# Layer 0 of a four-layer convolution network: loads written into the expansion, and the convolution's own patch on array tiles of 64 rows by 32 columns

## The chip, the cores and the metric

The kernel runs on one core of a Trainium2 chip. The metric is the device time in microseconds (us) of the whole kernel, which computes four layers one after the other. Only layer 0 is changed, and in the trace its blocks lie between about 147 and 4060 us of 6624. All data are fp32.

## The reference, cut to what matters

The input is `x` of shape (4, 64, 256, 256). Layer 0 adds to it the following function of its group-normalised self. Layers 1 to 3 are not touched.

```python
x = jnp.einsum('bchw,oc->bohw', x, w_in)              # 64 -> 384 channels
xp = patches of 8 x 8 of x
xp = jnp.fft.irfft2(jnp.fft.rfft2(xp) * fft_filter)   # per channel and patch
x = lax.conv_general_dilated(x, w_dw, 3 x 3, padding 1, feature_group_count=C)
x1, x2 = jnp.split(x, 2, axis=1)
x = jax.nn.gelu(x1, approximate=False) * x2
return jnp.einsum('bchw,oc->bohw', x, w_out)          # 192 -> 64 channels
```

The filter of a patch and the 3 x 3 convolution are linear and per channel. So the kernel does both in one go: each output pixel of a patch is a sum over the 64 pixels of its own patch, and for pixels at two edges over some pixels of the neighbour patches.

## The kernel before

**Tiling.** A block is 11 rows of patches of one image; there are three blocks to an image and 12 in all (`blocks`, index `p`). Within a block the 384 hidden channels are taken in four quarters (`kb`). For each quarter two stages follow each other on PE.

**Expansion** (`expand`, lines L444 and L450): for each of up to 12 rows of patches (`t`) PE computes the quarter's channels into PSUM tiles `psu`, with pixels of a patch on the partitions, and ACT and DVE copy them into the SBUF tile `u` (L459 to L463). There is one `u`, so the convolution starts when the last row is copied.

**Convolution** (`convolve`, twelve groups `g` of four channel pairs): the own patch (L494) is a matmul of 64 rows by 64 columns, two row halves `h` by two column halves `c`, four array tiles at a time, moving 374 columns. Then three units (`UNITS`: 16, 28 and 4 columns; L503) add the neighbour patches, in tiles of 64 by 32, eight at a time. An fp32 matmul appears as two MATMUL and two LDWEIGHTS instructions in the trace. ACT takes the Gelu of one half (L510), DVE multiplies by the other (L511), and the POOL queue stores the product `h` to DRAM tile `g` (L514).

**Projection** (`project`, L591 with 128 by 64 tiles, then L598 with 64 by 64): sixteen units of the block before, (row `r` of a patch, half), are woven into the convolution: four to a quarter, one `unit()` each after groups 1, 4, 7 and 10. Each needs tiles `g1` and `g6` from DRAM (`load_g`, L546 and L550), and each `r` needs the residual rows (`load_r`, L559). A `unit()` projects and right after it calls `load_half` for the next `r`. Pools of two buffers each hold `g1`, `g6` and `r`.

**Order.** PE, DVE, ACT and SP run in the order in which the program is written (`manual_schedule`); each queue for itself[...]. SP issues all loads: the convolution weights (`load_w`, L471, one tile for two groups, three pairs ahead, four buffers), the halves, the next image's statistics tiles (`load_stats`, L627, and `next_stats`, bn_stats at L320), and the next block's input rows (`load_x`, L418, then `normalize_x` at L256). Statistics and input tiles share a pool of four buffers. The statistics tiles are loaded in the first three quarters after every third group; the first four input rows stand after the last group of the third quarter, the others among the groups of the fourth.

**Weights.** At the start POOL writes the 64 by 112 tables of each channel to DRAM tiles `wts`, of which `load_w` fetches four channel pairs at a time.

## Time and profile before

| | |
|---|---|
| median of 3 runs | 6649.44 us (6638.31 to 6666.61) |
| profiled execution, its time | 6626.21 us |
| its span | 6624.4 us |
| mean granted TensorE clock | 0.953 |
| PE busy | 6040.5 us, 106712 matmuls |
| instructions in all | 238282 |
| DMA packets of queue 8 (instructions) | 843, 13.81 MB |
| own patch (L494): matmuls, mean | 9216, 494 ns |
| neighbour units (L503): matmuls, mean | 27648, 483 ns |

"PE" is the matmul side of TensorE and "PEld" its weight loads. Matmuls on different array tiles overlap, so a mean of 494 ns is not the time that one takes away from the next: the distance between starts is. The share of busy time counts overlapping matmuls once.

### The profile page before, as it was taken

How to read it: one execution, taken by the hardware profiler on the slowest of the kernel's cores; microseconds unless marked ns; L12 is line 12 of the kernel's file. 1: busy time of each engine (PE TensorE's matmuls, PEld its weight loads, DVE VectorE, ACT ScalarE, POOL GpSimd, SP SyncE). 2: the span in 40 equal slices, each digit the busy share in tenths (PEclk: the TensorE clock that was granted, in tenths of full speed). 3: DMA queues.
4: the chain of work that ended last, by engine and by line, in shares of the span. 5: the costliest groups of instructions: out<-in, count | busy, mean ns of one | idle time of the engine just before them, and what ended most of it. 6: DMA issues, size and time to landing. Idle time of an engine off the chain costs nothing.

```text
span 6624.4 us, 238282 instructions
## 1 busy us (share of the span) xinstructions
PE 6040.5 (91%) x106712; PEld 3213.7 (49%) x106712; DVE 4275.7 (65%) x5924; ACT 3238.8 (49%) x4564; POOL 1050.4 (16%) x1646
## 2 busy tenths in 40 slices
PE   2999999999999999999999986999899999999987
PEld 1455555555555555555555543333344444443576
DVE  5556555555555555555555545999798898885355
ACT  4454434344434444344444422777777887783211
POOL 3111111111111111111111111111022222221011
PEclk9999999999999999999999997999999999999855
DMA  8577777777878877877767669999666666677889
GB/s 236 152 206 211 216 213 222 218 216 213 230 213 238 219 222 207 223 214 220 210 193 206 188 194 247 232 229 228 165 177 176 168 180 173 173 187 264 318 351 394
DMA packets 878510, 1447.67 MB, mean 219 GB/s; under 512 B 77252, under 2 KB 586452, under 8 KB 875444
## 3 DMA queue, kind: packets, MB, share of 16 engines
q1 hardware_dynamic: 725284, 923.09, 54.8%
q0 software_dynamic: 148672, 500.14, 21.7%
q8 instruction: 843, 13.81, 0.9%
q10 hardware_dynamic: 3536, 9.20, 0.5%
q14 instruction: 175, 1.43, 0.1%
HBM read 932.08 MB, written 500.04 MB: 216 GB/s over the span
## 4 chain that ended last, share of the span: by engine, by line
PE 82%; DMA 6%; ACT 5%; DVE 3%; issue 3%; SPq 0%; POOL 0%; ACTq 0%; DVEq 0%; POOLq 0%
PE pc L503 18%; PE pc L494 12%; PE m L869 10%; PE psu L444 9%; PE one L1110 8%; PE div L1069 6%; PE po L591 4%; ACT u L459 4%; PE psu L450 4%; PE psz L1099 2%; PE po L598 2%; DMA x<-x 2%; PE psa L1297 2%; DMA g<-g 2%; PE psy L1444 1%
## 5 line engine op out<-in xcount | busy, mean ns | idle before, releaser
L511 DVE TENSOR_TENSOR h<-h,pc 128x374 f32<-128x374 f32 x1152 | 574.7, 541 | 1268.7 <-ACT h L510 1267.7
L510 ACT ACTIVATE h<-pc 128x374 f32<-128x374 f32 x1152 | 492.6, 480 | 1824.9 <-PE pc L503 1822.0
L503 PE MATMUL pc<-u,w 64*16 64x374 f32 (+2 forms) x27648 | 1244.1, 483 | 0.0
L494 PE MATMUL pc<-u,w 64*64 64x374 f32 x9216 | 928.6, 494 | 81.1 <-DVE u L463 32.2
L514 POOL DMA_DIRECT2D g<-h x576 | 416.7, 723 | 3111.0 <-DVE h L511 2904.7
L503 PEld LDWEIGHTS pc<-u,w 64*16 64x16 f32 (+2 forms) x27648 | 413.8, 92 | 769.5 <-issue 768.9
L444 PE MATMUL psu<-win,xn 64*128 64x96 f32 x8704 | 627.0, 283 | 131.8 <-ACT u L459 110.5
L459 DVE COPY u<-psu 64x384 f32<-64x384 f32 x1088 | 604.3, 555 | 167.7 <-PE psu L444 155.7
L459 ACT COPY u<-psu 64x384 f32<-64x384 f32 x1088 | 560.0, 515 | 238.9 <-PE psu L444 218.8
L444 PEld LDWEIGHTS psu<-win,xn 64*128 64x128 f32 x8704 | 574.0, 192 | 202.6 <-ACT u L459 143.6
L1055 DVE TENSOR_TENSOR q<-xn 128x2313 f32<-128x2313 f32 (+2 forms) x256 | 627.4, 2492 | 1.7 <-ACT xn L256 1.7
L1110 PE MATMUL one<-z,wp 32*32 32x512 f32 x16384 | 592.1, 596 | 17.8 <-issue 13.6
L494 PEld LDWEIGHTS pc<-u,w 64*64 64x64 f32 x9216 | 350.3, 133 | 531.0 <-issue 354.7
L256 ACT ACTIVATE xn<-x,nb,r 128x1024 f32<-128x1024 f32 (+3 forms) x272 | 486.8, 1793 | 244.6 <-DMA x<-x 140.8
L1056 ACT ACTIVATE q<-q 128x2313 f32<-128x2313 f32 (+2 forms) x256 | 529.0, 2086 | 32.7 <-DVE q L1055 31.2
L450 PE MATMUL psu<-win,xn 64*64 64x96 f32 x17408 | 458.2, 252 | 81.9 <-issue 57.2
L1069 PE MATMUL div<-q,ones 64*32 64x512 f32 x8192 | 466.3, 594 | 12.9 <-ACT q L1056 9.3
L1110 PEld LDWEIGHTS one<-z,wp 32*32 32x32 f32 x16384 | 367.6, 103 | 223.6 <-issue 80.1
L450 PEld LDWEIGHTS psu<-win,xn 64*64 64x64 f32 x17408 | 395.5, 137 | 126.0 <-issue 77.0
L1143 POOL DMA_DIRECT2D x<-r x512 | 275.5, 547 | 969.8 <-DVE r L1140 945.1
L591 PE MATMUL po<-g,wo 128*64 128x176 f32 (+1 forms) x3072 | 315.8, 348 | 63.3 <-DMA g<-g 41.3
L869 PE MATMUL m<-t,wk 64*64 64x512 f32 x3072 | 341.1, 588 | 0.0
(162 smaller groups left out, 6668.1 us busy)
## 6 DMA issues: line engine op xcount, KB each, us to landing
g<-h POOLq DMA_DIRECT2D x576, 374.0 KB, 7.0
x<-x SPq DMA_DIRECT2D x240, 640.0 KB, 6.4
w<-wt SPq DMA_DIRECT2D x288, 448.0 KB, 8.4
x<-x SPq DMA_DIRECT2D x100, 1024.0 KB, 14.2
g<-g SPq DMA_DIRECT2D x414, 187.0 KB, 5.7
g<-g SPq DMA_DIRECT2D x736, 93.5 KB, 6.0
x<-in_x_dram SPq DMA_DIRECT2D x256, 256.0 KB, 8.1
x<-o POOLq DMA_DIRECT2D x128, 512.0 KB, 8.2
```

The lines of the kernel that those rows point to most:

```text
L444: nc.tensor.matmul(ps[s][:, k, at], xn[halves[s], n : n + 2].rearrange("p n r w -> p (n r w)"), win[halves[s], kb, 0 : 2 * PB], start=True ...
L450: nc.tensor.matmul(ps[s][halves[1 - odd], k, at], xn[halves[s], n + odd].rearrange("p r w -> p (r w)"), win[halves[s], kb, PB * (1 - odd) ...
L459: copy(at(h, 8 * s + o), v[k, c : c + PB])
L494: nc.tensor.matmul(out(C * c, C, k, h), w[halves[h], k, 2 * (G % 2) + c, 0:C], cells(h, 4 * g + 2 * k + c, 0, 0), start=True, stop=False, ...
L503: nc.tensor.matmul(out(q, m, k, h), w[halves[h], k, 2 * (G % 2) + c, c0 : c0 + m], cells(h, 4 * g + 2 * k + c, down, right), start=False, ...
L511: nc.vector.tensor_mul(h[:, k], h[:, k], ps[k][:, 1, 0:L])
L591: nc.tensor.matmul(out(k, s, x), wo1, moving(g1[:, 2 * k], 2 * half + k, s, x), start=(x == 0), stop=False, skip_group_check=True,)
L869: nc.tensor.matmul(rows2(m)[halves[j], s], w[dx][halves[s]], ts[n][halves[s], i, 2 * j : 2 * j + 2, dx : dx + W], start=(dx == 0), stop=(d ...
L1055: nc.vector.tensor_sub(d, p0, p1)
L1056: nc.scalar.activation(d, d, AF.Square)
L1069: ins = nc.tensor.matmul(ps[quarters[j], h], ones[halves[h]], q[n, g, k][halves[h], r + 2 * j : r + 2 * j + 2, o : o + W], start=(m == 0), ...
L1110: ins = nc.tensor.matmul(rows2(ps[g])[quarters[j], k], w[quarters[i]], z[quarters[i], h, 2 * j + dy : 2 * j + dy + 2, dx : dx + W], tile_p ...
```

## The change

- The own patch is computed in twice as many matmuls of 32 columns each, with a loop over the column half `q`, so that all of the convolution uses tiles of 64 by 32.
- The weight tiles in DRAM and SBUF hold the two phases `k` of a channel next to each other: a partition of `load_w` reads one run of 4 x 2 x 112 values where it read two runs of 4 x 112.
- Projection units stand after groups 0, 3, 6 and 9. After the first two, the next half is loaded at once; after the other two it is put on a list `later` and loaded in the program text of the next expansion, after its rows 7 and 9. The first halves of a block (written ahead of its first expansion so far) go the same way.
- In the expansions of the first three quarters, up to four statistics tiles are loaded after rows 8 to 11; in that of the fourth, the first four input rows. `next_stats` runs after odd groups.
- The last pass, which only projects the last block, loads as before.

```diff
-        wts = [dr.tile([2, 64, 2, Q, NC], F32, name=f"wt{t}") for t in range(HID // C)]
+        wts = [dr.tile([2, 64, Q, 2, NC], F32, name=f"wt{t}") for t in range(HID // C)]
...
-            w = wl[j] = p_w.tile([128, 2, 4, NC], F32, tag="w", name=f"w_{j}")
+            w = wl[j] = p_w.tile([128, 4, 2, NC], F32, tag="w", name=f"w_{j}")
             nc.sync.dma_start(
-                w, wts[k // 8][:, :, :, 4 * (k % 8) : 4 * (k % 8) + 4].rearrange("h i k c n -> (h i) k c n")
+                w, wts[k // 8][:, :, 4 * (k % 8) : 4 * (k % 8) + 4].rearrange("h i c k n -> (h i) c k n")
             )
...
             for k in range(2):
-                for c in range(2):
-                    for h in range(2):
-                        nc.tensor.matmul(
-                            out(C * c, C, k, h), w[halves[h], k, 2 * (G % 2) + c, 0:C], cells(h, 4 * g + 2 * k + c, 0, 0),
-                            start=True, stop=False, tile_position=(h * C, c * C), skip_group_check=True,
-                        )
+                for q in range(2):
+                    for c in range(2):
+                        for h in range(2):
+                            at = C * c + Q * q
+                            nc.tensor.matmul(
+                                out(at, Q, k, h), w[halves[h], 2 * (G % 2) + c, k, Q * q : Q * q + Q],
+                                cells(h, 4 * g + 2 * k + c, 0, 0),
+                                start=True, stop=False, tile_position=(h * C, at), skip_group_check=True,
+                            )
...
-                ahead = 1
+                ahead, later = 1, []
...
                 for r in range(ahead):
                     for half in range(2):
-                        load_half(p - 1, r, half)
-
-                def unit():
+                        later.append((p - 1, r, half))
+                        if p == NB:
+                            load_half(*later.pop())
+
+                def unit(wait=False):
                     at = next(units, None)
                     if at:
                         project(p - 1, *at)
-                        load_half(p - 1, at[0] + ahead, at[1])
+                        later.append((p - 1, at[0] + ahead, at[1]))
+                        if not wait:
+                            load_half(*later.pop(0))
...
                     for t in range(NR + 1):
                         if 0 <= i0 + t < NP:
                             expand(p, kb, t)
+                        if t in (7, 9) and later:
+                            load_half(*later.pop(0))
+                        if t >= 8:
+                            if kb == 3 and t - 8 < len(fresh):
+                                load_x(fresh[t - 8])
+                            elif kb < 3 and nk:
+                                loaded.append(nk.pop(0))
+                                load_stats(b + 1, loaded[-1])
...
-                        if g in (1, 4, 7, 10):
-                            unit()
+                        if g in (0, 3, 6, 9):
+                            unit(wait=g > 3)
                         if kb < 3:
-                            if g % 3 == 0:
-                                if len(loaded) == 2 or not nk:
-                                    for k in loaded[: 1 if nk else 2]:
-                                        next_stats(b + 1, loaded.pop(0))
-                                if nk:
-                                    k = nk.pop(0)
-                                    load_stats(b + 1, k)
-                                    loaded.append(k)
-                            if kb == 2 and g == NG - 1:
-                                for row in fresh[:4]:
-                                    load_x(row)
+                            if g % 2 and loaded:
+                                next_stats(b + 1, loaded.pop(0))
```

More of the change, by code (lines that the diff above doesn't have):

```diff
@@ L395, in weights @@
                             nc.gpsimd.dma_start(
-                                wts[t][h, 32 * hh : 32 * hh + 32, k, :, n0 : n0 + n].rearrange("i c n -> c i n"),
+                                wts[t][h, 32 * hh : 32 * hh + 32, :, k, n0 : n0 + n].rearrange("i c n -> c i n"),
                                 T[quarters[2 * h + k], :, :, c0 : c0 + n].rearrange("p a b n -> p (a b) n"),
@@ L503, in convolve @@
                             nc.tensor.matmul(
-                                out(q, m, k, h), w[halves[h], k, 2 * (G % 2) + c, c0 : c0 + m],
+                                out(q, m, k, h), w[halves[h], 2 * (G % 2) + c, k, c0 : c0 + m],
                                 cells(h, 4 * g + 2 * k + c, down, right),
```

## The prediction

> **What bounds the kernel now.** I read the page first: its busy table, its chain, its groups. Then the order of time inside one block of layer 0, then the waits of PE and of the SP queue, and last the DMA share in stretches of 4 us.

> ```profile
> PE 6040.5 (91%) x106712; PEld 3213.7 (49%) x106712; DVE 4275.7 (65%) x5924; ACT 3238.8 (49%) x4564; POOL 1050.4 (16%) x1646
> ...
> PE pc L503 18%; PE pc L494 12%; PE m L869 10%; PE psu L444 9%; PE one L1110 8%; PE div L1069 6%; PE po L591 4%; ACT u L459 4%; PE psu L450 4%; PE psz L1099 2%; PE po L598 2%; DMA x<-x 2%; PE psa L1297 2%; DMA g<-g 2%; PE psy L1444 1%
> ```

> PE is the bound, and the two lines of the convolution, L494 (own patch) and L503 (neighbour units), are 30% of the chain. Groups of the page: L503 has 27648 matmuls, L494 9216; that is 48 and 16 for each of 576 groups (12 blocks, 4 quarters of the channels, 12 groups). All of it lies between 146.6 and 3937 us. One group of the convolution in the timeline of all engines:

> ```profile
> 1500.65 1.52 PE L494 MATMUL pc<-u,w 64*64 64x374 f32 x16
> ...
> 1501.02 0.16 PEld L494 LDWEIGHTS pc<-u,w 64*64 64x64 f32 x4 [0.16 <-PE pc L503]
> ...
> 1501.33 0.17 PEld L494 LDWEIGHTS pc<-u,w 64*64 64x64 f32 x4 [0.15 <-issue]
> 1502.10 0.15 PEld L503 LDWEIGHTS pc<-u,w 64*16 64x16 f32 x16 [0.60 <-issue]
> 1502.10 2.16 PE L503 MATMUL pc<-u,w 64*16 64x374 f32 x48
> ...
> 1503.08 0.13 PEld L503 LDWEIGHTS pc<-u,w 64*4 64x4 f32 x8 [0.17 <-issue]
> 1503.40 0.13 PEld L503 LDWEIGHTS pc<-u,w 64*4 64x4 f32 x8 [0.19 <-issue]
> ...
> 1504.20 1.53 PE L494 MATMUL pc<-u,w 64*64 64x374 f32 x16
> ```

> The first column is the start. A group lasts 1504.20 - 1500.65 = 3.55 us. Its matmuls run in rounds: four at a time on tiles of 64 by 64 (4 rounds), eight at a time on tiles of 64 by 32 (6 rounds). Consecutive bursts of weight loads are 0.31 to 0.33 us apart, so (1503.40 - 1502.10) / 4 = 0.325 us is a round. Ten rounds are 3.25 us; the missing 0.30 us stand at the two seams: 1.45 us from the first L494 to the first L503, where four rounds are 1.30, and 2.10 us to the next group, where six are 1.95. So **a seam costs 0.15 us**, and PE waits for nothing else there. Now the waits of PE, the longest of the SP queue, and the DMA share (last but one column) around one expansion, which began at 1200.5 and gave way to the convolution at 1226:

> ```profile
> PE psu L444 <- ACT u L459: 110.5, 171, 1.5
> ...
> PE psu L450 <- issue: 57.2, 48, 4.2
> ...
> PE psu L444 <- issue: 18.7, 23, 1.8
> ...
> SPq L546 <- PE po L591: 1280.3, 117, 32.5
> ...
> 1208.00:1212.00 4.00, 2.53 (x82) 2.25 (x78) 3.09 (x6) 3.49 (x8) 0.00 (x0) 1.00 1.07 262
> ...
> 1216.00:1220.00 4.00, 2.92 (x56) 2.66 (x60) 2.82 (x6) 2.60 (x6) 0.00 (x0) 1.00 0.03 7
> ...
> 1228.00:1232.00 4.00, 3.83 (x36) 1.35 (x44) 0.02 (x1) 0.00 (x0) 0.00 (x0) 0.60 0.00 0
> ...
> 1268.00:1272.00 4.00, 4.00 (x76) 1.47 (x72) 1.00 (x2) 1.02 (x3) 0.73 (x1) 1.00 1.06 323
> ```

> The DMA engines are full through the convolution and the first 16 us of the expansion, then empty for some 20 us, because SP stands at L546 for a buffer that the next projection frees. The convolution waits for no load: its groups follow each other without idle time. The expansion does wait: for ACT's copies, and 71 times (48 + 23) for "issue", 75.9 us in all, none of them in the convolution.

> [...] a seam at each change of 64 by 64 to 64 by 32, of 0.15 us, and none between the three units[...]. [...] The page's queue 8 agrees on the size (843 packets, 13.81 MB; PE's 213,424 instructions are 253 to a packet); I read the "issue" waits as late blocks[...]. [...] The stretch 1228:1232 above has a granted clock of 0.60 after PE waited for the last copies[...].

> **The change part by part.**
> 1. *Own patch on tiles of 64 by 32.* It takes 32 instructions of each kind per group where there were 16 (fp32 matmuls stand twice in the trace), eight at a time: again four rounds. Bounds of a round 0.31 (own now) and 0.33; I take the units' 0.325. Of a convolution phase with four projections (44 of 48): eight own parts fall from 1.45 to 1.30, four that follow a projection from 1.41 (1509.82 to 1511.23) to 1.30, seven unit parts that run into the next group from 2.10 to 1.95. That is 1.20 + 0.44 + 1.05 = 2.69 us. Against it, L598 of the projection is itself 64 by 64, so the own part after it gets a seam that it didn't have: 4 x 0.17 = 0.68 (the first own round after a seam is 0.02 us longer). After an expansion the new seam lies under the wait for the last copies (L494 waits there 1 to 2 us anyway). Net 2.0 us; 44 x 2.0 = 88. The four phases of block 0 have no projection: 23 seams x 0.15 = 3.45, x 4 = 14. **Sum 102 us less.**
> 2. *9216 matmuls and 9216 weight loads more.* Their time is in the rounds; their fetching isn't. A group asks for 160 instructions in 3.25 us, 49 a us, where it was 128 in 3.55, 36 a us. The expansion runs at about 192 in 3.5 us, 55 a us, between its waits, and there late blocks cost 75.9 us over some 53,000 instructions, 0.36 us a block. From below: nothing, as now. From above: the expansion's price, 8.6 blocks x 0.36 = 3.1 us a phase, 137 us over 44 phases. I take 0.9 us a phase, 40 us: the rate is nearer the expansion's than to the old one, but the next step takes load off the DMA engines in these phases. **40 us more.**
> 3. *Loads moved.* Two of four half loads of a phase (1.12 MB each, every other with 0.7 MB of residual rows) and the four statistics tiles (0.5 MB each) are written after the ninth group now instead of among the groups. SP's order is only that of its own queue: nothing in it waits for the expansion's rows, so "second half" is where they stand in the text. They will issue as soon as the weight load of the eleventh group has its buffer, about 9 us before the expansion starts; the buffers that they need (g1, g6, r, x) are free by then. That is 9 us before, up to some 15 us after the start of the expansion: the stretch that is full today. Queued behind them on SP is the weight load of the next first group, due six groups later, over 20 us. The POOL queue keeps its stores and waits for none of these. The convolution loses nearly 2.2 + 0.7 + 2 MB of some 16. PE waits on no load today in these phases, so the move alone gains nothing; that projections start one group earlier finds their tiles landed (6 to 8 us to landing, a whole expansion before use). In the last of the four quarters the four x tiles stood at the same place of SP's order already. Bounds for the expansions: later statistics loads may add 1 us to each (+44), a shorter queue may take 1 us away (-44). I take 0. DVE's statistics at odd groups: 1.28 us beside 1.1 us of products in 3.25 us, and after a half 1 also some 3.3 us of projection work in 5.5: covered.
> 4. *Weight layout.* The same bytes, one run of 3584 B per partition instead of two of 1792. Loads are three pairs of groups ahead (8.4 us to landing); 0, or a little DMA time back. The table writes keep their run lengths: 0.

> Sum: -102 + 40 = -62. The profiled execution took 6626.2 us around a span of 6624.4, 23 us under the median of the three runs (6649.4), so its counterpart is 6564, and for the median 6649 - 62 = **6587**.

> **Rivals.**
> - *The fetch stays hidden and the expansions recover* (0.16). For it: the DMA queue in the convolution is shorter. Against: it carries h stores and weight loads all the same. 102 + up to 30: about 6520 to 6550.
> - *Instruction fetch becomes the bound of the convolution* (0.17), the slower side. Place: all 44 phases with projections. It decides when a block of 256 takes longer than 256 / 49 = 5.2 us under load. For it: median landings of 6 to 8 us for other transfers in the page; the late blocks of the expansion. Against: no such wait today at 7.1 us a block. Price: the expansion's 0.36 us a block gives 137 - 102 = +35; with all that the expansions lose (by their starts in the timeline 11 rows take 23.6 us and 12 rows 26.2 where nothing disturbs them; all 47 together take some 120 us more, over 209 blocks) 0.6 a block, 227 - 102 = +125. So 6684 to 6775.
> - *The change doesn't do what it says* (0.15). Either the eight weight loads of an own round keep the rounds from packing (own back at 1.45), so that only the seven seams into the next group go, or the loads stay bunched and the fetch eats most of the gain: 6625 to 6660.

> **How the numbers follow.** Likeliest (0.52): 6587, with its own range 6540 to 6625 from half to one and a half times the terms of 40 and of the expansions. The full range reaches into the first rival and into the low end of the slower one: 6500 to 6690. A measurement of this kernel can tell about 0.5%, 33 us, from no change; below 6616 lie most of the likeliest and the first rival: 0.61; within 33 us a part of the likeliest and most of the last: 0.22; above, 0.17.

> **What would show it.** Step 1: L494 64 columns gone, 18432 matmuls of 32, a group of 3.2 to 3.3 us, L598 to L494 longer by 0.15. Step 2: about 73 more packets on queue 8 and "issue" among the waits of L494 and L503, some 40 us. Step 3: SP's loads at the start of the expansion, the DMA share still near zero in its last 10 us, and the wait at L546 shorter. The forecast is wrong if the group stays at 3.5 us, if "issue" in the convolution is over 100 us, or if PE waits for g at a phase's first projection.

## The result, and the profile after

The changed kernel is slower: 6716.31 us median of 4 runs (6701.14 to 6729.94) against 6643.88 us for the kernel before, a ratio of 1.0101 (95% interval 1.0074 to 1.0128). The forecast was 6587 us, with 6690 as its upper end. The profiled execution took 6729.94 us around a span of 6728.2, 104 us more than that of before. The medians are 72 us apart: the profiled execution of before was 18 us under its median, this one 14 over. What follows on single stages is read from this pair of executions, so it adds up to 104 and not to 72.

The page, with the busy table, the chain and the instruction queue:

```profile
PE 6048.6 (90%) x115928; PEld 3620.6 (54%) x115928; DVE 4282.5 (64%) x5924; ACT 3243.7 (48%) x4564; POOL 1046.6 (16%) x1646
...
q8 instruction: 915, 14.99, 1.0%
...
PE pc L506 17%; PE pc L496 12%; PE m L875 10%; PE psu L444 9%; PE one L1116 9%; PE div L1075 7%; PE psu L450 4%; PE po L594 4%; ACT u L459 4%; PE po L601 2%; PE psz L1105 2%; DMA x<-x 2%; PE psa L1303 2%; DMA g<-g 1%; PE psy L1450 1%
```

PE is busy for nearly the same time as before with 9216 matmuls more (the own patch is L496 now, the units L506, the projection L594 and L601), and queue 8 moved 72 packets more. An undisturbed stretch of the convolution, in the timeline of PE (start, duration, line, forms, count):

```profile
1509.20 1.53 PE L496 MATMUL pc<-u,w 64*32 64x374 f32 x32
1510.48 2.16 PE L506 MATMUL pc<-u,w 64*16 64x374 f32 x48
1512.40 1.53 PE L496 MATMUL pc<-u,w 64*32 64x374 f32 x32
1513.66 2.19 PE L506 MATMUL pc<-u,w 64*16 64x374 f32 x48
1515.58 1.58 PE L496 MATMUL pc<-u,w 64*32 64x374 f32 x32
1516.84 2.28 PE L506 MATMUL pc<-u,w 64*16 64x374 f32 x48
1519.05 1.46 PE L594 MATMUL po<-g,wo 128*64 128x160 f32 x16
1520.44 0.85 PE L601 MATMUL po<-g,wo 64*64 64x160 f32 x16
1521.22 1.54 PE L496 MATMUL pc<-u,w 64*32 64x374 f32 x32
```

From one L496 to the next are 3.20 and 3.18 us where it was 3.55: **the seams are gone**. So the loss is elsewhere. The waits of PE (in total, times, longest), with one line of the SP queue:

```profile
PE psu L450 <- issue: 100.3, 76, 3.3
PE psu L444 <- ACT u L459: 93.0, 150, 0.9
...
PE pc L506 <- issue: 35.5, 31, 3.1
...
PE psu L444 <- issue: 30.2, 23, 3.4
...
PE pc L496 <- issue: 23.9, 19, 2.1
...
SPq L549 <- PE po L594: 1095.2, 88, 24.4
```

"issue" has come into the two lines of the convolution and has grown in the expansion's two from 75.9 to 130.5 us. What one such wait does is seen in the fourth quarter of one block:

```profile
1989.38 0.88 PE L450 MATMUL psu<-win,xn 64*64 64x96 f32 x29
1993.34 1.86 PE L450 MATMUL psu<-win,xn 64*64 64x96 f32 x35 [3.09 <-issue]
1995.13 3.73 PE L444 MATMUL psu<-win,xn 64*128 64x96 f32 x32
2000.88 3.22 PE L496 MATMUL pc<-u,w 64*32 64x374 f32 x32 [2.02 <-DVE u L459]
2003.34 3.95 PE L506 MATMUL pc<-u,w 64*16 64x374 f32 x48
...
2050.32 1.13 PE L496 MATMUL pc<-u,w 64*32 64x374 f32 x17
2052.11 0.56 PE L496 MATMUL pc<-u,w 64*32 64x374 f32 x8 [0.66 <-issue]
...
2055.93 1.79 PE L506 MATMUL pc<-u,w 64*16 64x374 f32 x32
2058.98 0.85 PE L506 MATMUL pc<-u,w 64*4 64x374 f32 x15 [1.25 <-issue]
```

PE stands in the middle of a row for 3.09 us; then the same 32 matmuls of L444 that take 2.03 us elsewhere (at 1982.94, for instance) take 3.73, and after the wait for DVE's copies the units take 3.95 instead of 2.2. The clock goes with that. The same expansion in stretches of 4 us (the last three columns are granted clock, DMA share and GB/s):

```profile
1987.00:1991.00 4.00, 3.01 (x61) 2.72 (x61) 3.47 (x7) 3.31 (x7) 0.00 (x0) 1.00 1.14 207
1991.00:1995.00 4.00, 1.66 (x35) 1.57 (x35) 0.73 (x2) 0.48 (x1) 0.00 (x0) 0.74 0.60 98
1995.00:1999.00 4.00, 3.86 (x35) 3.49 (x32) 1.74 (x4) 1.59 (x4) 0.00 (x0) 0.50 0.00 0
```

The DMA engines are full (a share of 1.14), PE stands, and then the clock is halved (0.50).

The trace itself supports reading these waits as late instruction blocks. Queue 8 moved 915 packets of 16,384 bytes each, and PE's 234,284 instructions in the trace (matmuls, weight loads and its sequencer's own) are 256 to a packet. The wait above ended at 1993.34 us, 1.58 us after such a packet had ended at 1991.76. Of the 153 "issue" waits in the two stages of layer 0, 151 end 1.2 to 1.8 us after the end of a packet of queue 8; of 20,000 random moments, 9% do, and of the 223 waits for other causes, 5%. And all 153 stand at the same place in PE's program: the number of these instructions that PE had started is the same modulo 256, to within 2. In the kernel before it is so for all 71 (70 of them at that distance from a packet).

The fourth quarter of that block as a whole, before (two lines) and after (two lines), expansion and convolution in turn:

```profile
1931.50:1959.00 27.50, 20.73 (x520) 18.87 (x513) 22.71 (x42) 20.80 (x41) 1.23 (x2) 1.00 0.88 193
1959.00:2013.40 54.40, 53.98 (x900) 22.62 (x900) 21.40 (x40) 20.65 (x33) 11.55 (x16) 0.97 0.85 224
```

```profile
1965.70:2000.90 35.20, 24.85 (x514) 22.71 (x514) 22.36 (x41) 20.73 (x41) 0.71 (x1) 0.84 0.84 193
2000.90:2059.80 58.90, 55.49 (x1092) 30.27 (x1092) 20.84 (x35) 20.87 (x33) 12.60 (x16) 0.95 0.91 245
```

By the starts of the stages in the timelines, the mean length of a stage in blocks 1 to 11 (in the fourth quarter 1 to 10), in us:

| quarter | expansion before | after | convolution before | after | "issue" in it after |
|---|---|---|---|---|---|
| first | 26.5 | 26.9 | 52.9 | 53.2 | 0.9 |
| second | 27.4 | 28.8 | 52.8 | 51.5 | 0.0 |
| third | 26.9 | 28.0 | 53.7 | 52.0 | 0.2 |
| fourth | 28.7 | 32.1 | 53.6 | 59.4 | 4.9 |

Over all stages but the last convolution and its tail: expansions 1319 to 1394 us (+75), convolutions 2466 to 2491 (+25). The sum, 100, is nearly the whole of the 104. "Issue" in them went from 76 to 131 us and from 0 to 66. The length of the half clock times one half, which is the most that it can have cost, went from 61 to 140 us (by the clock records of the traces, which hold full speed and 0.5 of it and nothing else). The waits and the clock overlap with waits that were there anyway, for instance for ACT's copies (110 to 93 us for L444), so they don't add up exactly.

### The profile page after: what moved, and what is told of

It reads as the page before. It is cut to its first block, busy times and chain, and to the rows that moved or that the text cites. A ratio compares the mean times of both kernels' runs of the same rounds, so it can differ in the third digit from the quotient of the medians.

```text
span 6728.2 us, 256613 instructions
## 1 busy us (share of the span) xinstructions
PE 6048.6 (90%) x115928; PEld 3620.6 (54%) x115928; DVE 4282.5 (64%) x5924; ACT 3243.7 (48%) x4564; POOL 1046.6 (16%) x1646
## 4 chain that ended last, share of the span: by engine, by line
PE 82%; DMA 5%; ACT 4%; issue 4%; DVE 3%; SPq 0%; POOL 0%; ACTq 0%; DVEq 0%; POOLq 0%
PE pc L506 17%; PE pc L496 12%; PE m L875 10%; PE psu L444 9%; PE one L1116 9%; PE div L1075 7%; PE psu L450 4%; PE po L594 4%; ACT u L459 4%; PE po L601 2%; PE psz L1105 2%; DMA x<-x 2%; PE psa L1303 2%; DMA g<-g 1%; PE psy L1450 1%
## 5 line engine op out<-in xcount | busy, mean ns | idle before, releaser
L506 PE MATMUL pc<-u,w 64*16 64x374 f32 (+2 forms) x27648 | 1378.8, 487 | 35.9 <-issue 35.5
L496 PE MATMUL pc<-u,w 64*32 64x374 f32 x18432 | 991.3, 491 | 101.3 <-DVE u L463 32.4
L506 PEld LDWEIGHTS pc<-u,w 64*16 64x16 f32 (+2 forms) x27648 | 714.0, 93 | 493.3 <-issue 153.3
L444 PE MATMUL psu<-win,xn 64*128 64x96 f32 x8704 | 637.7, 288 | 127.4 <-ACT u L459 93.0
L459 DVE COPY u<-psu 64x384 f32<-64x384 f32 x1088 | 603.9, 555 | 196.6 <-PE psu L444 184.5
L444 PEld LDWEIGHTS psu<-win,xn 64*128 64x128 f32 x8704 | 584.0, 197 | 196.2 <-ACT u L459 122.8
L459 ACT COPY u<-psu 64x384 f32<-64x384 f32 x1088 | 561.1, 516 | 263.6 <-PE psu L444 243.6
L496 PEld LDWEIGHTS pc<-u,w 64*32 64x32 f32 x18432 | 433.6, 106 | 444.7 <-issue 176.3
L450 PE MATMUL psu<-win,xn 64*64 64x96 f32 x17408 | 484.1, 258 | 129.8 <-issue 100.3
L256 ACT ACTIVATE xn<-x,nb,r 128x1024 f32<-128x1024 f32 (+3 forms) x272 | 486.6, 1792 | 172.6 <-DMA x<-x 138.2
L450 PEld LDWEIGHTS psu<-win,xn 64*64 64x64 f32 x17408 | 415.9, 141 | 181.2 <-issue 127.9
L594 PE MATMUL po<-g,wo 128*64 128x176 f32 (+1 forms) x3072 | 317.1, 348 | 67.3 <-DMA g<-g 37.1
```

The costliest lines, as they stand in the source:

```text
L444: nc.tensor.matmul(ps[s][:, k, at], xn[halves[s], n : n + 2].rearrange("p n r w -> p (n r w)"), win[halves[s], kb, 0 : 2 * PB], start=True ...
L450: nc.tensor.matmul(ps[s][halves[1 - odd], k, at], xn[halves[s], n + odd].rearrange("p r w -> p (r w)"), win[halves[s], kb, PB * (1 - odd) ...
L459: copy(at(h, 8 * s + o), v[k, c : c + PB])
L496: nc.tensor.matmul(out(at, Q, k, h), w[halves[h], 2 * (G % 2) + c, k, Q * q : Q * q + Q], cells(h, 4 * g + 2 * k + c, 0, 0), start=True, s ...
L506: nc.tensor.matmul(out(q, m, k, h), w[halves[h], 2 * (G % 2) + c, k, c0 : c0 + m], cells(h, 4 * g + 2 * k + c, down, right), start=False, ...
L594: nc.tensor.matmul(out(k, s, x), wo1, moving(g1[:, 2 * k], 2 * half + k, s, x), start=(x == 0), stop=False, skip_group_check=True,)
```

## The experiments

All of them are read by the time, by "issue", and by the same means of stages. **F** is the theory that PE's instruction blocks arrive late because it asks for more instructions in less time while the DMA engines are full.

**The tiles alone.** The kernel before with the new own patch, and nothing else:

```diff
-                            out(C * c, C, k, h), w[halves[h], k, 2 * (G % 2) + c, 0:C], cells(h, 4 * g + 2 * k + c, 0, 0),
...
+                for q in range(2):
...
+                                out(at, Q, k, h), w[halves[h], k, 2 * (G % 2) + c, Q * q : Q * q + Q],
```

> The kernel before with one edit, the own patch on tiles of 64 by 32; all loads, units and the weight layout stay. Theory F (instruction fetch: at 49 instructions a us in the convolution the 256-instruction blocks arrive late while the DMA engines are full): the group takes 3.2 us, but 'issue' appears on the two lines of the convolution, spread over all four quarters since the loads still stand among the groups; total between 6620 and 6780, 'issue' in the convolution over 60 us. Rival M (the moved loads cause the loss, the tiles alone gain): 6540 to 6570, 'issue' in the convolution under 20 us.

Measured: 6773.85 us, ratio 1.0197 (1.0169 to 1.0225). The two lines of the convolution:

```profile
PE pc L506 <- issue: 70.8, 64, 3.1
...
PE pc L496 <- issue: 47.8, 37, 2.6
```

"Issue" stands in the convolutions of every quarter now (2.5, 3.0, 1.4 and 4.5 us each), which take 56.1, 56.5, 53.6 and 59.0 us; the expansions are unchanged in sum (1318). Rival M falls. The tiles alone are worse than the whole change: the moved loads pay for part of what the tiles cost.

**The moves alone.** The changed kernel with the own patch on 64 by 64:

```diff
-                for q in range(2):
...
-                                out(at, Q, k, h), w[halves[h], 2 * (G % 2) + c, k, Q * q : Q * q + Q],
...
+                            out(C * c, C, k, h), w[halves[h], 2 * (G % 2) + c, k, 0:C], cells(h, 4 * g + 2 * k + c, 0, 0),
```

> The changed kernel with the own patch back on tiles of 64 by 64: loads, units and weight layout as changed. Theory F: no more than the kernel before within 0.4% (6620 to 6670), expansions together within 25 us of before (1318 us), no 'issue' in the convolution. Rival M: expansions keep the 75 us that they gained in the changed kernel, and the saving of the seams is missing: 6710 to 6800.

Measured: 6666.2 us, ratio 1.0034 (1.0022 to 1.0045). Convolutions as before (2468), expansions 1351 us, 32 more; F had allowed 25. Some 26 of the 32 are in the second quarter's expansions (27.4 to 29.8 us). The medians differ by 19 us only, so 32 is rather too much. The moves have a price of their own, in the expansions:

```profile
PE psu L450 <- issue: 81.0, 68, 3.9
PE psu L444 <- issue: 19.8, 23, 2.7
```

**The old weight layout.** The changed kernel with the layout of `wts` and `load_w` as before, here the line of the SBUF tile:

```diff
-            w = wl[j] = p_w.tile([128, 4, 2, NC], F32, tag="w", name=f"w_{j}")
+            w = wl[j] = p_w.tile([128, 2, 4, NC], F32, tag="w", name=f"w_{j}")
```

> The changed kernel with the weight layout of before: two runs of 1792 B per partition instead of one of 3584. Theory F: the bytes are the same, so within 0.3% of the changed kernel (6695 to 6735). Rival L (longer packets hold up the instruction blocks on the DMA engines): 6580 to 6660, with 'issue' waits of PE below those of the changed kernel by a half.

Measured: 6726.86 us, ratio 1.0132 (1.0108 to 1.0155), its interval meeting that of the change. No effect of the length of these packets is shown; rival L, with 6580 to 6660, falls. The run also shows how well stages repeat: its expansions take 1390 us in sum and its convolutions 2497, against 1394 and 2491, but single quarters differ by up to 1.0 us.

**Instructions without new tiles.** The kernel before, each own matmul cut along the moving side:

```diff
-                for c in range(2):
+                for i0, i1 in ((0, 6), (6, NR)):
+                    for c in range(2):
...
-                            out(C * c, C, k, h), w[halves[h], k, 2 * (G % 2) + c, 0:C], cells(h, 4 * g + 2 * k + c, 0, 0),
+                                out(C * c, C, k, h)[:, i0:i1], w[halves[h], k, 2 * (G % 2) + c, 0:C],
+                                cells(h, 4 * g + 2 * k + c, 0, 0, i0, i1),
```

> The kernel before, with each own matmul of 64 by 64 issued as two over 6 and 5 of the 11 rows (204 and 170 moving columns): the same array time and seams, but 16 matmuls and 16 weight loads more per group, as many as the change adds. Group of 3.6 us, 160 instructions, 45 a us. Theory F: 'issue' in the convolution 20 to 90 us where before had none, expansions longer by 20 to 60 us, total 6680 to 6800. If the count of instructions doesn't matter: 6630 to 6670 and no 'issue' in the convolution.

Each half starts a sum of its own here (`start=True`), and the values that come out are other ones (a relative error of 0.16); how that comes about was not shown. Measured: 6789.11 us, ratio 1.0219 (1.02 to 1.0238), and where the convolution had no "issue":

```profile
PE pc L505 <- issue: 44.8, 48, 3.1
PE pc L495 <- issue: 28.2, 27, 2.5
```

Same tiles, same seams, same loads: more instructions, with nothing else changed, make the blocks late. The halves themselves cost nothing: in the first three quarters of block 0, where no projection is woven in, the convolutions take 44.4 to 45.0 us, against 44.4 before. This is the cleanest of the runs for F. In one point F was wrong: it had expected expansions longer by 20 to 60 us, and they took 1296, 22 less than before.

**Half of the seams for no instruction.** The kernel before with groups in pairs; `convolve` now issues own(g), own(g+1), units(g), units(g+1):

```diff
-                        convolve(p, kb, g)
+                            convolve(p, kb, (g, g + 1))
...
-                        if g in (1, 4, 7, 10):
+                        if g in (1, 3, 7, 9):
```

> The kernel before with the groups in pairs: own patches of g and g+1 (64 by 64), then the units of g and g+1, then ACT and DVE as before; projections after groups 1, 3, 7 and 9. It has half of the seams and not one instruction more. Theory F (the change lost by its instructions, the seams were priced right): six pairs save two seams of 0.15 us each, 1.8 us a phase and 86 us over 48 phases, with 256 instructions in 6.8 us still 38 a us and no 'issue' in the convolution: 6550 to 6590. Rival N (the seam isn't what it looked like, or four PSUM tiles in use at once make PE wait for ACT and DVE between pairs): 6630 to 6700, with PE waiting for h at the start of pairs.

Measured: 6685.58 us, ratio 1.007 (1.0046 to 1.0094): a miss. The order does what it should:

```profile
1528.64 2.75 PE L496 MATMUL pc<-u,w 64*64 64x374 f32 x32
1531.32 4.06 PE L507 MATMUL pc<-u,w 64*16 64x374 f32 x96
1535.31 2.82 PE L496 MATMUL pc<-u,w 64*64 64x374 f32 x32
1538.06 4.12 PE L507 MATMUL pc<-u,w 64*16 64x374 f32 x96
```

A pair takes 1535.31 - 1528.64 = 6.67 us where two groups took 7.10, there is no wait between pairs, and "issue" in the convolution is 11 us. But the convolutions gave back only 18 us in all, and the expansions became 102 us longer in the profiled execution: "issue" there went from 76 to 110 us, and half of the half clock's length from 35 to 113 us. That execution was 33 us over the median of its runs, and the one of before 18 under: the two are 92 us apart and the medians 41, so the 102 is rather too much as well. So rival N's mechanism is not what happened either. Time gained in the convolution was lost again in the expansion, with PE's program of the same length.

**The fourth quarter without its later input rows.** The changed kernel; rows from the fifth on are normalised from the first four tiles:

```diff
-                            if k + 4 < len(fresh):
-                                load_x(fresh[k + 4])
+                            if k >= 4:
+                                x0[fresh[k]] = xk[k % 4]
```

> The changed kernel without the loads of the input rows from the fifth on in the fourth quarter (rows of the next block are normalised again from the first four tiles, so the values of later rows are not theirs). All instructions of PE stay. Theory F with full DMA engines as the cause of late blocks: the fourth quarter's convolution falls from 59.4 us to between 51 and 54 and its 'issue' from 4.9 us to under 1.5; total 6610 to 6665. If it is the count of instructions alone, whatever the DMA engines do: 58 to 60 us there, total 6690 to 6725.

Measured: 6609.35 us, ratio 0.994 (0.9918 to 0.9963). The fourth quarter's convolution fell from 59.4 to 51.2 us and its "issue" from 4.9 to 0.04 us, with the mean DMA share in it down from 0.92 to 0.69 (0.85 in the kernel before). The same instructions at the same rate: it takes both, the rate and the full DMA engines. The total is no gain of the change, since loads are missing that the kernel before has. Of its waits in the profile one line of the convolution is left near the top, with

```profile
PE pc L506 <- issue: 7.1, 9, 2.2
```

The expansions stayed at 1398 us.

**The fourth quarter on 64 by 64.** The changed kernel with the old own patch where the input rows are loaded:

```diff
+                if kb == 3:
...
+                            out(C * c, C, k, h), w[halves[h], 2 * (G % 2) + c, k, 0:C],
...
+                    continue
                 for q in range(2):
```

> The changed kernel with the own patch on tiles of 64 by 64 in the fourth quarter only. Theory F: no 'issue' in the fourth quarter's convolution, 53 to 54.5 us there as before, the other three as in the changed kernel; 11 x 5.5 = 60 us less than the changed kernel: 6640 to 6675, no better than before because the expansions keep what the moved loads cost. Rival (the loss of the fourth quarter comes from the moved loads and not from the tiles): 57 us or more there, 6690 to 6725.

Measured: 6649.69 us, ratio 1.0004 (0.9991 to 1.0018); the fourth quarter's convolution 53.7 us, without "issue". So the loss there belongs to the tiles on these loads, not to the moved loads. What the seams save in the other three quarters (convolutions 2412 us, 54 under before) is eaten by the expansions (1394 us, 75 over).

**Half of the moved loads put back.** On top of the last kernel:

```diff
-                            unit(wait=g > 3)
+                            unit(wait=g > 6)
...
-                            elif kb < 3 and nk:
+                            elif kb < 3 and nk and t in (8, 10):
...
-                            if g % 2 and loaded:
+                            if g in (1, 3, 9, 11) and loaded:
                                 next_stats(b + 1, loaded.pop(0))
+                            if g in (5, 7) and nk:
+                                loaded.append(nk.pop(0))
+                                load_stats(b + 1, loaded[-1])
```

> The changed kernel with the own patch on 64 by 64 in the fourth quarter, and with half of the moved loads put back among the groups: the half after group 6 loads at once, two of the four statistics tiles load after groups 5 and 7 (bn_stats after 1, 3, 9 and 11). In the changed kernel the DMA engines are full from 8 us before the expansion to 22 us after its start, and half empty from 20 to 8 us before it. Theory F: the full stretch ends 4 us earlier, the expansions give back 25 to 45 us of the 75 that they lost, the first three convolutions lose under 20: 6610 to 6650, ratio 0.994 to 1.000. Rival (the expansions are long for another reason than the moved loads): they stay at 1390 us together and the total at 6640 to 6670.

Measured: 6717.26 us, ratio 1.0106 (1.0083 to 1.0128): a miss. The convolutions of the first three quarters got their "issue" back, 1.98 to 2.44 us each,

```profile
PE pc L515 <- issue: 34.2, 29, 3.0
...
PE pc L505 <- issue: 20.9, 18, 3.9
```

and grew to 55.1, 54.5 and 54.1 us. The expansions fell only to 1372 us, although their "issue" fell to 84 us and the DMA engines were full for the first 13 us of the second and third instead of 21 to 24 (by the packets of the trace). Half of the half clock's length was still 93 us there, 87 in the changed kernel. So a longer full stretch alone doesn't explain the longer expansions.

**Without the later statistics loads.** The changed kernel; statistics tiles of the second and third quarter are those of the first again:

```diff
+                                if kb == 0:
                                     load_stats(b + 1, loaded[-1])
+                                else:
+                                    st[b + 1, loaded[-1]] = st4[loaded[-1] % len(st4)]
```

> The changed kernel with the statistics tiles loaded only in the first quarter of each block; the others are taken from those tiles again, so the statistics of the second to fourth image are not theirs. PE's instructions stay. Theory F with the DMA engines full in the expansion: the expansions of the second and third quarter fall from 28.8 and 28.0 us to between 25.5 and 27 with 'issue' there halved (26 to 28 us each to under 15), the fourth's stays above 30; total 6670 to 6700. If the tiles of the own patch alone make the expansions late: no shift beyond 0.7 us in either.

Measured: 6686.69 us, ratio 1.0067 (1.0042 to 1.0091), 30 us under the change, though the two intervals still touch. The second quarter's expansion fell from 28.8 to 27.4 us, the third's not at all (28.1), and "issue" in the two went from 28.4 and 26.0 us to 22.0 and 29.2. Half a hit: these loads may cost something in the second quarter, but most of the expansions' loss isn't theirs.

## Why the prediction was wrong

The forecast was 62 us less, and layer 0 of the profiled pair took 100 more. The 162 us between fall on three terms: the seams 24 (78 saved, not 102), the fetch in the convolution 63 (103 lost, not 40, because the convolutions end 25 us longer in spite of the seams), and the expansions 75 (taken as 0). By the medians the miss is smaller, 72 + 62 = 134 us. So two terms failed: **the 40 of step 2 was mis-sized, and the 0 of step 3 was wrong outright and beyond its bound of 44.**

- **Step 1, the seams: right in kind, a quarter too large.** A group takes 3.18 to 3.20 us. The first two phases of block 0, undisturbed, fell from 44.4 to 40.8 us (3.6; the working had 3.45). Undisturbed phases with projections gave less than the 2.0 us forecast: in block 10 the second and third fell from 52.5 to 51.2 and 50.9. The own part after a projection starts 0.80 us after L601 instead of 0.68 after L598, but the units before a projection also take longer, 2.12 to 2.21 us where it was 2.06; that was not in the sum. 44 x 1.45 + 4 x 3.6 is some 78 us, not 102.
- **Step 2, the fetch: right in kind, wrong in size.** I took 40 us between 0 and 137 and argued that the moved loads relieve the convolution. They do, in the second and third quarter: 0.2 us of "issue" at most, and with the tiles alone 3.0 and 1.4 us each. But I spread one price over all 44 phases. The input rows of the fourth quarter stay among its groups, and there "issue" is 4.9 us a phase and the stage 5.8 us longer. That the DMA engines are full through the convolution was too coarse a reading: their mean share was 0.79 to 0.82 in the first three quarters and 0.85 in the fourth. The run without those rows and the one with the old tiles in that quarter both take that loss away. The price was also too low for what a late block does: the forecast's larger figure, 0.6 us a block with all that follows, stood in the rival that ends slower.
- **The clock.** It was quoted in the prediction with the stretch at 0.60 and then left out of the sum. Half of its length is 79 us more than before, at most that much was lost to it, and that is as much as the seams save.
- **Step 3, the moves: wrong, and the largest miss.** I took 0 between -44 and +44 for the expansions; they are 75 us longer, and with the moves alone 32. The moves did shift the traffic: the DMA engines are full until 21 to 24 us after the start of the second and third expansion, not until 15, and they are half empty from 20 to 8 us before it. That this is what costs the 32 us isn't shown: with the moves alone the third expansion has the same full stretch and isn't longer (26.7 us, 26.9 before). That SP isn't held by the expansion's rows was right: the burst starts 8 us before the stage, and SP's wait for a projection fell from 1280 to 1095 us.
- **Step 4, the layout: right.** No difference shown (6726.86 us with the old one, 6716.31 with the new).
- **The rivals.** "Instruction fetch becomes the bound" is the one that happened in the convolution, given 0.17, with late blocks as it wrote (that a block takes over 5.2 us was not shown) and its place too wide: the fourth quarter rather than all phases. Its 6684 to 6775 holds the result, but in part by luck: it left the expansions as they were, and 75 of the 100 us stand there. That convolution phases follow each other without idle time today was read as slack; it was a margin of unknown size.

What stays open is part of the expansions' 75 us. The moves account for 32 at most. The rest needs neither more instructions nor loads moved into the expansion: the pairs have neither, and their expansions are 102 us longer. It doesn't appear with the tiles alone or the cut matmuls, whose convolutions are much slower. Late blocks are later in the long expansions (waits of 2 us or more: 7 before, 22 after, 17 with pairs, 10 with the tiles alone). Why they are later with pairs, no run shows; the DMA engines are full for some 15 us of the second and third expansion there, as before. Late blocks aren't all of it either: in the pairs' first expansions "issue" is 17.1 us in blocks 1 to 11 where it was 15.5, but each takes 30.5 us instead of 26.5, and half of the half clock's length is 30 us where there was none.

## What to carry to other kernels

A saving on the bounding engine that is bought with more instructions has to be priced at the instruction queue as well: count instructions per microsecond, look for "issue" waits in the stage with the next higher rate, and look at what fills the DMA engines in each stage, not on average. A stage without such waits has a margin, not a guarantee; 36 instructions a microsecond went unpunished here; 45 brought 73 us of "issue" into the convolutions; 49 brought 4.9 us a phase at a mean DMA share of 0.92 and 0.04 us at 0.69. And before a stage's time is counted as saved, look at the stage next to it: in the run with the old tiles in the fourth quarter it took back all that the convolutions had saved (54 us saved, 75 lost).
